# Two graph layers on one core: the start of layer 0's chain of norms, and the lead of layer 0 over layer 1

## The chip, the cores and the metric

The kernel runs on one core of one Trainium2 chip. The metric is the device time of one execution in microseconds (us); the time before is the median of three runs. Engines are named as in the profile: PE (matrix products), PEld (its weight loads), DVE (vector), ACT (scalar, activation functions), POOL and SP.

## The reference

The input `x` has 16 batches of 1024 rows of 256 values, `adj` 16 matrices of 1024 x 1024. Two layers follow each other, each wrapped in a residual and a norm. Cut to what matters here:

```python
# layer 0: 4 heads of 64 values
h = einsum('bnd,hde->bhne', x, W)
weight = sum over t of (adj == t+1) * (e_src[t] + e_dst[t])     # from h, a_src, a_dst
attention = softmax(where(adj == 0, -1e9, leaky_relu(weight)))
out = relu(attention @ h + bias) + h
out = layernorm over each head's 64 values
x = layernorm(x + out)
# layer 1: 8 heads of 32 values, no projections
n = layernorm(x)                      # gamma1, beta1
a = softmax(where(adj > 0, n n^T / sqrt(32), -inf)) @ n
x1 = x + a
mlp = gelu(layernorm(x1) @ W1 + b1) @ W2 + b2          # 256 -> 1024 -> 256
x = layernorm(x + (x1 + mlp))
```

Everything is in float32. Row b of `x` goes through both layers alone, so layer 0 of batch b+1 and layer 1 of batch b are independent.

## The kernel before

**Two streams.** `fast_path` is written as two Python generators, `layer0()` and `layer1()`, each of which runs over the 16 batches. A generator records instructions for the engines and then yields a cost in units of its own. Instructions of an engine run in the order in which they are recorded, so the order of these turns is the order of the work. A loop at the end of `fast_path` picks whose turn is next: layer 0's, if its place (batch plus fraction done, in units of `WORK0` = 47) is less than `wanted()`, otherwise layer 1's. `wanted()` reads a table, `COURSE`: for every point of layer 1's batch b (`ATTN1` = 82 units of attention, then 56 units of MLP up to `WORK1` = 138) it says how far layer 0 should be. It goes from 1.0 (batch b+1 not begun) to 2.0 (batch b+1 done), with 1.54 at the end of the attention, and 2.0 is reached 22 units ahead of the end of the MLP.

**Layer 0, a batch of it.** `prepare` loads rows in pairs of blocks of 128, transposes them (line 227), turns the adjacency into masks (lines 295 and 296) and makes the projections (line 322): 13 units. `attention0` runs 16 steps, (half n of the queries, head, half of the keys), of 2 units each. A step records its products (line 389, into a PSUM tile `acc`) and then the weights of the next step (line 374, into `p0`, four buffers, two a step). After a head's second step (`j4 == NB - 4`) its tail is due: `relu_residual` (lines 418 to 430).

**The chain of norms.** With a half's last head (head 3), `after0` goes on from `relu_residual` to the norms of these 512 rows. It is a chain of ten more parts, each of which waits for a number of units before it is recorded, so that its results are ready:

1. load of `xl`; sum and mean off, lines 445 and 446 (DVE)
2. squares `sq`, line 451 (ACT)
3. variances `v0s`, lines 454 and 455; the power `r0` on POOL, line 198; lines 457 and 458 (DVE)
4. scaling and residual, lines 460 and 461 (DVE)
5. statistics, lines 203 and 204, and `v2`, lines 469 and 470 (DVE); a second power on POOL
6. `t` and `ratio`, lines 208, 475 and 476 (DVE)
7. scaled rows into `sq` again, line 214 (ACT)
8. `x1`, line 484 (DVE); the first transposes, line 227 (PE), into `nT`, line 233 (ACT)
9. the second transposes, likewise
10. `v1`, line 494 (DVE)

`begin(chain, wait)` hangs a chain up at the running clock plus `wait`; `advance(cost)` moves the clock after each turn of either stream and runs the parts that are due. `complete(chain)` runs all that is left of one at once, without the pauses between the parts. `half(n)` in `layer1` calls it through `finish_norms` when layer 1 asks for half n of its batch, as only then must `x1`, `v1` and `nT` exist. Half 1 is asked for at the fifth step of a batch's attention.

**Layer 1, a batch of it.** `attention1` runs 32 steps of 2.5 units: scores (line 517), exponentials (line 522, ACT), one step later their masking (line 528, DVE), two steps later the products (lines 535 and 542). `heads_out` (lines 577 to 593) and `finish1` (lines 604 to 613) follow behind as chains. `mlp` runs four chunks of eight hidden blocks (lines 637 and 644, in pairs of 1.75 units) and eight output blocks (line 650, 3.5 units), each with a `last_norm` that adds the output block into `z` (line 680) and so frees one of two `po` tiles.

## Time and profile before

| what | value |
|---|---|
| median of three runs (lowest, highest) | 3886.35 us (3886.32, 3887.58) |
| span of the profiled run | 3880.2 us |
| mean granted TensorE clock | 0.957 |
| PE, PEld busy | 3451.0 us (89%), 2319.4 us (60%) |
| DVE, ACT, POOL busy | 2994.8 us (77%), 2151.8 us (55%), 388.3 us (10%) |
| HBM traffic over the span | 31 GB/s |
| chain that ended last, by engine | PE 64%, DVE 23%, issue 7%, POOL 3%, ACT 2%, DMA 1% |

Busy shares are means over the whole span. The kernel repeats one pattern, a batch of layer 1 beside the next batch of layer 0, fifteen times; between the start (layer 0 alone on the first batch) and the end (layer 1 alone on the last). One repetition takes about 237 us, so a microsecond in it is worth fifteen in the total. What limits the kernel differs from one part of the pattern to the next, so it is read with the timeline and with windows cut to those parts, not from the shares.

### The profile page before, as it was taken

The page shows a single profiled execution, that of the slowest core. Times are in us where ns is not written, and L with a number is a line of the kernel's source. Part 1 is how long each engine was busy: PE and PEld are TensorE (multiplying, and loading weights), DVE is VectorE, ACT ScalarE, POOL GpSimd, SP SyncE. Part 2 cuts the span into 40 slices and gives each one's busy share as a digit, 9 for nine tenths or more (in the row PEclk, how much of TensorE's full clock was granted, in tenths as well). Part 3 has the DMA queues.
Part 4 walks back from the last instruction along what each step waited for, and adds up shares of the span by engine and source line. Part 5 has one row for each costly group of instructions (what it writes and reads, how often), then busy time and mean ns, then how long its engine had stood idle before and what let it go on. Part 6 is the DMA issues. An engine that isn't in the chain of part 4 may idle for free.

```text
span 3880.2 us, 141934 instructions
## 1 busy us (share of the span) xinstructions
PE 3451.0 (89%) x64417; PEld 2319.4 (60%) x64417; DVE 2994.8 (77%) x5328; ACT 2151.8 (55%) x4732; POOL 388.3 (10%) x360
## 2 busy tenths in 40 slices
PE   5799898989989899898998989989898998989988
PEld 4457475565746657465584755747556574665746
DVE  4787796878868787797877968779687786878784
ACT  2564646647465464755646556464654746547454
POOL 0101001010110101101011010100101011010100
PEclk9799999999999999999999999999999999999999
DMA  4100101011020110201002010010101102010000
GB/s 100 34 14 23 35 12 41 8 31 27 13 44 4 34 25 15 43 4 38 19 18 40 11 37 14 23 35 12 41 8 31 27 13 44 4 31 14 14 6 13
DMA packets 77669, 97.67 MB, mean 25 GB/s; under 512 B 9088, under 2 KB 60160, under 8 KB 77056
## 3 DMA queue, kind: packets, MB, share of 16 engines
q0 software_dynamic: 18432, 33.56, 5.9%
q1 hardware_dynamic: 52736, 50.35, 4.2%
q8 instruction: 506, 8.29, 0.9%
q10 hardware_dynamic: 5888, 4.60, 0.4%
q14 instruction: 107, 0.88, 0.1%
HBM read 105.26 MB, written 16.78 MB: 31 GB/s over the span
## 4 chain that ended last, share of the span: by engine, by line
PE 64%; DVE 23%; issue 7%; POOL 3%; ACT 2%; DMA 1%; ACTq 0%; POOLq 0%; DVEq 0%
PE ps L517 14%; PE po L650 9%; PE acc L389 9%; PE po L535 9%; PE ps L637 8%; DVE p L374 7%; DVE p L528 6%; PE po L542 5%; PE acc L322 3%; POOL r L198 2%; PE acc L227 2%; DVE st L203 1%; PE acc L295 1%; PE ps L363 1%; DVE relu L421 1%
## 5 line engine op out<-in xcount | busy, mean ns | idle before, releaser
L528 DVE TENSOR_TENSOR p<-p,mask 128x1024 f32<-128x1024 f32 x1024 | 1199.0, 1221 | 175.0 <-ACT p L522 174.4
L522 ACT ACTIVATE p<-ps 128x512 f32<-128x512 f32 x2048 | 1058.8, 614 | 366.8 <-PE ps L517 364.8
L517 PE MATMUL ps<-nT 32*128 32x512 f32 x4096 | 748.6, 665 | 12.5 <-ACT cb L365 10.0
L374 DVE SCALAR_TENSOR_TENSOR p<-cb,dinv,mask 128x512 f32<-128x512 f32 x1024 | 698.9, 746 | 0.5 <-ACT cb L365 0.5
L389 PE MATMUL acc<-v,p 128*64 128x65 f32 x16384 | 577.9, 230 | 89.7 <-DVE p L374 87.4
L389 PEld LDWEIGHTS acc<-v,p 128*64 128x64 f32 x16384 | 532.6, 143 | 151.0 <-issue 102.4
L542 PEld LDWEIGHTS po<-v,p 128*32 128x32 f32 x32768 | 386.7, 109 | 326.5 <-issue 242.8
L535 PE MATMUL po<-p,v 128*32 128x512 f32 x2048 | 547.1, 609 | 25.0 <-DVE p L528 25.0
L535 PE MATMUL po<-p,unit 128*32 128x512 f32 x2048 | 546.6, 609 | 0.0
L637 PE MATMUL ps<-yT,w_sb 128*128 128x256 f32 x2048 | 480.3, 384 | 0.1
L650 PE MATMUL po<-w_sb,hid 128*128 128x256 f32 x2048 | 467.1, 383 | 0.0
L644 ACT ACTIVATE hid<-ps,b_sb 128x256 f32<-128x256 f32 x512 | 230.3, 471 | 380.8 <-PE ps L637 379.4
L650 PEld LDWEIGHTS po<-w_sb,hid 128*128 128x128 f32 x2048 | 389.5, 191 | 54.6
L637 PEld LDWEIGHTS ps<-yT,w_sb 128*128 128x128 f32 x2048 | 377.8, 190 | 73.1 <-issue 23.1
L542 PE MATMUL po<-v,p 128*32 128x33 f32 x32768 | 384.6, 198 | 2.2
L517 PEld LDWEIGHTS ps<-nT 32*128 32x128 f32 x4096 | 254.7, 191 | 154.7 <-ACT p L522 51.0
L535 PEld LDWEIGHTS po<-p,v 128*32 128x32 f32 x2048 | 78.2, 108 | 408.5 <-DVE p L528 219.0
L680 DVE TENSOR_TENSOR z<-po,x 128x256 f32<-128x256 f32 x128 | 54.1, 423 | 319.0 <-PE po L650 319.0
L198 POOL TENSOR_TENSOR r<-v,mhalf 128x1 f32<-128x1 f32 (+1 forms) x160 | 140.2, 877 | 1084.9 <-DVE v L684 616.0
L227 PE MATMUL acc<-ident,sq 128*128 128x128 f32 x136 | 37.0, 447 | 222.2 <-ACT sq L214 221.0
L214 ACT ACTIVATE sq<-hb,t,r 128x256 f32<-128x256 f32 x128 | 66.5, 590 | 256.3 <-DVE t L208 158.2
L198 POOL TENSOR_TENSOR r<-v1s,mhalf 128x4 f32<-128x4 f32 x32 | 54.4, 1701 | 1282.0 <-DVE v1s L609 1282.0
(116 smaller groups left out, 3149.5 us busy)
## 6 DMA issues: line engine op xcount, KB each, us to landing
ak<-in_adj_dram POOLq DMA_DIRECT2D x128, 256.0 KB, 3.8
xk<-in_x_dram SPq DMA_DIRECT2D x64, 256.0 KB, 2.7
xl<-in_x_dram SPq DMA_DIRECT2D x32, 512.0 KB, 3.9
out_dram<-z SPq DMA_DIRECT2D x128, 128.0 KB, 1.7
w_sb<-in_L_gnn_W_dram ACTq DMA_DIRECT2D x2, 1024.0 KB, 10.3
v<-in_L_gnn_a_src_dram ACTq DMA_DIRECT2D x1, 640.0 KB, 9.0
v<-in_L_gnn_a_dst_dram ACTq DMA_DIRECT2D x1, 640.0 KB, 3.8
w0e<-in_L_gnn_W_dram ACTq DMA_DIRECT2D x8, 32.0 KB, 7.7
```

What stands on the lines that cost most here:

```text
L198: nc.gpsimd.tensor_tensor(r, src, mhalf[:, :n], op=OP.pow)
L322: nc.tensor.matmul(ph, xT[:, c, g * P : (g + 1) * P], w0e[:, c, :], start=c == 0, stop=c == DC - 1)
L374: nc.vector.scalar_tensor_tensor(p[:, i, :], cb[:, hd % PAIR, :], dinv[:, j2 + i, hd : hd + 1], mask[n][:, j2 + i, :], op0=OP.max, op1=OP. ...
L389: nc.tensor.matmul(av[at : at + TILE, q, :], ps[i // 2][:, i % 2, q * P + at : q * P + at + TILE], v0[:, j4 + i, hd, :], start=j4 + i == 0 ...
L517: nc.tensor.matmul(tiles[e], of_keys[q, quad, keys], of_queries[q, quad, :], start=True, stop=True)
L522: nc.scalar.activation(p[:, i, :], tiles[e + i], AF.Exp, scale=SCALE1)
L528: nc.vector.tensor_mul(p, p, mask[n][:, jb, None, :].to_broadcast([P, PAIR, HALF]))
L535: nc.tensor.matmul(moved[at * Q : (at + 1) * Q, :], v, ps[0][:, e, :], start=jb == 0, stop=jb == NB - 1)
L542: nc.tensor.matmul(held[at : at + Q, q, e, :], ps[1][:, e, q * P + at : q * P + at + Q], values[:, hd, :], start=jb == 0 and e == 0 and q ...
L637: nc.tensor.matmul(ph, w1_sb[:, c, f * P : (f + 1) * P], yT[:, c, q * P : (q + GB) * P], start=c == 0, stop=c == DC - 1,)
L644: nc.scalar.activation(hid[f // 4][:, f % 4, :], ph, AF.Gelu, bias=b1_sb[:, f : f + 1], scale=1.0)
L650: nc.tensor.matmul(po, hid[f // 4][:, f % 4, g * P : (g + 1) * P], w2_sb[:, f, :], start=f == 0, stop=f == FC - 1,)
```

## The change

```diff
@@ attention0
             if j4 == 0 and i + 3 < len(steps) and hd % PAIR == PAIR - 1:
                 g = steps[i + 3][0], steps[i + 3][1] // PAIR
                 cbs[g] = spread_factor(*g)
-            yield 2.0
             if j4 == NB - 4:
                 norms[b, n, hd] = after0(b, n, hd, av, hb[n], rinv[:, n * BPH : (n + 1) * BPH, :])
-                begin(norms[b, n, hd], 0.0)
+                begin(norms[b, n, hd], 2.5)
+            yield 2.0
@@ fast_path
-    COURSE = [(0.0, 1.0), (ATTN1, 1.54), (WORK1 - 22.0, 2.0), (WORK1, 2.0)]
+    COURSE = [(0.0, 1.0), (ATTN1, 1.45), (WORK1 - 14.0, 2.0), (WORK1, 2.0)]
```

The first part moves the point at which a head's tail is hung up from the head of layer 0's next turn to the turn of the head's last products. The wait of 2.5 counts from the clock ahead of that turn's own 2.0 units, so the tail is recorded after whichever turn follows. The purpose is that the chain of the last head is not left until layer 0 is next given a turn.

The second part changes when layer 0 gets its turns. It is to be at 1.45 instead of 1.54 of its batch when layer 1's attention ends, and to be done 14 units ahead of the end of the MLP instead of 22. The instructions themselves, their number and their sizes stay as they are; only their order changes.

## The prediction

> **What bounds the kernel now.** I read the list of waits first, sorted by total, and looked only at PE rows, because PE has the largest busy share (89%). One row stands out; its columns are total us, times, longest us:

> ```profile
> PE acc L227 <- ACT sq L214: 221.0, 17, 15.6
> ```

> PE waits at the transposes of line 227 for the scaled rows `sq` (line 214), the seventh part of layer 0's chain of norms. Two of the 17 waits (7.27 and 9.62 us) belong to the start of the run, the other 15 to the fifteen changes from one batch of layer 1 to the next: 204 / 15 = 13.6 us each. The timeline of PE at one such change (start, duration, then the idle time in brackets):

> ```profile
> 619.63 0.62 PE L295 MATMUL acc<-identb,ak 128*128 128x128 bf16 x8
> 633.72 2.17 PE L227 MATMUL acc<-ident,sq 128*128 128x128 f32 x8 [13.47 <-ACT sq L214]
> 635.81 2.09 PE L517 MATMUL ps<-nT 32*128 32x512 f32 x8
> ```

> PE stands from 620.2 to 633.7 and then runs slowly: the four products of line 517 take 2.09 us here and 1.14 us a few microseconds later. What DVE does in that hole:

> ```profile
> 620.66 1.22 DVE L454 TENSOR_REDUCE v0s<-sq 128x16 f32<-128x1024 f32 x1
> 621.91 0.17 DVE L455 TENSOR_SCALAR v0s<-v0s 128x16 f32<-128x16 f32 x1
> ...
> 626.04 1.23 DVE L460 TENSOR_TENSOR hb<-hb,r 128x1024 f32<-128x1024 f32 x1 [1.33 <-POOL r L198]
> ...
> 632.86 0.16 DVE L208 SCALAR_TENSOR_TENSOR t<-mv,r 128x4 f32<-128x4 f32 x1 [1.80 <-POOL r L198]
> ...
> 636.93 4.63 DVE L528 TENSOR_TENSOR p<-p,mask 128x1024 f32<-128x1024 f32 x4
> ```

> It is one serial chain with two powers on POOL in it, and the masking that layer 1 needs (line 528) is queued behind it. Then I cut one batch (236.8 us) into four stages by what PE runs, and read busy time per stage (PE, PEld, DVE, ACT, POOL, then clock, DMA):

> ```profile
> 607.50:694.30 86.80, 71.17 (x1511) 37.34 (x1510) 65.02 (x95) 66.03 (x168) 10.43 (x11) 0.92 0.24 48
> 694.30:757.50 63.20, 58.44 (x1531) 33.59 (x1532) 59.18 (x86) 33.41 (x66) 1.94 (x1) 0.97 0.01 3
> 757.50:819.60 62.10, 59.70 (x873) 50.81 (x874) 56.51 (x128) 26.00 (x45) 9.66 (x6) 1.00 0.06 17
> 819.60:844.30 24.70, 24.70 (x120) 21.53 (x120) 5.82 (x24) 9.21 (x18) 2.23 (x4) 1.00 0.05 17
> ```

> Stage 1 (layer 1's attention beside layer 0's preparation) is PE's, apart from the hole. Stage 2 (both attentions) is DVE's: 59.2 of 63.2 us. Stage 3 (MLP beside layer 0's attention) loads both. Stage 4 (MLP alone) is PE's, with DVE idle three quarters of the time:

> ```profile
> 828.83 0.42 DVE L680 TENSOR_TENSOR z<-po,x 128x256 f32<-128x256 f32 x1 [7.38 <-PE po L650]
> 834.01 0.42 DVE L680 TENSOR_TENSOR z<-po,x 128x256 f32<-128x256 f32 x1 [3.01 <-PE po L650]
> 840.92 0.42 DVE L680 TENSOR_TENSOR z<-po,x 128x256 f32<-128x256 f32 x1 [4.73 <-PE po L650]
> ```

> [...] 0.50 granted from 627 to 637. [...] masking waits behind the chain. [...] from 737 to 747 PE reads 10.0 of 10 busy, yet the chain that ended last runs through DVE there. So below I price PE by the pieces of that chain, not by busy time: line 517 1.07 us a step, lines 535 and 542 1.00 + 0.56, one product step of layer 0 (line 389) 2.02, a pair of hidden blocks (line 637) 1.73, one output block (line 650) 3.45, line 322 1.09.

> **The change, part by part.** (a) *Where the chain begins.* Before, the code behind `yield 2.0` runs at layer 0's next turn. For the last head of a batch there is none until layer 1 has begun its next batch: COURSE ends at exactly 2.0, and the test is a strict "less than". The lead of 22 units that COURSE leaves therefore passes with the chain not begun; it begins in the hole's own batch, and ten units later `half(1)` completes it by force, seven parts in a row. After, it begins in the turn of the last products; 2.5 units is one turn of layer 1 later. The order of instructions of the changed kernel, built, shows this: the reductions, `sq`, the first power and lines 457 to 461 stand in front of the batch's last `z`; the statistics stand behind the first two masking operations of the new batch; only from line 208 (`t`) on is it forced, four parts.

> Price: PE waits from the end of its second set of products (619.3, without line 295's 0.6, which now comes later) for `t` behind the third masking (620.8 by the hole's rows), four line 214 operations behind the exponentials (2.08 us, the first two are enough), four transposes and the first `nT` (0.5 to 1.0). That is 3.5 us idle; bounds 2 (masking earlier) and 5.5 (all four scalings wanted first). Saved: 13.5 - 3.5 = 10. Slow clock: line 227 2.17 against twice 0.6, line 517 2.09 against 1.14, line 535 1.52 against 1.00, together 2.4, of which I keep 0.4. **Sum -12 us a batch.** The 8.6 us of DVE passes (seven of 1.22) and 1.1 us of ACT move to stage 4. That becomes 3 x 1.73 + 3 x 3.45 = 15.5 us long by (c), with about 4.2 us of `z` work (three groups of 1.4) and one `relu` of 1.45 on DVE: 14.3 in all, which just fits: nothing. The first power (3.82 us) lies beside an output block and its `z` there: nothing.

> (b) *`relu_residual` of the other heads* comes after one turn of layer 1 instead of after layer 0's next turn. It is a wait on the products of its head, with masking or weights queued behind it. But the next weights need those same products, because `p0` has four buffers, two a step. No new wait; no cost.

> (c) *COURSE.* Layer 0 owes 0.45 x 47 = 21.2 units at the end of layer 1's attention instead of 25.4; after 15 units of preparation that is 4 steps of products instead of 6, and the built order has 4 and 6. Three steps of layer 1's attention pass from stage 2 to stage 1. In front of the next batch are left 3 pairs of hidden blocks and 3 output blocks, before 6 and 4.

> Stage 1: +3 x (1.07 + 1.56) + 0.6 for transposes (line 593) = **+8.5**; DVE has room there. Stage 2, by DVE: three maskings of 2.31, two sets of weights of 2.65, one `relu` of 1.45 and the first half's `finish1` (about 5.5 in the rows at 696 to 705, which the built order has ahead of stage 2) leave: 6.9 + 5.3 + 1.45 + 4.4 (some of it stays) = **-18**, to 45 us. PE's own sum there is 10 x 1.07 + 12 x 1.56 + 4 x 2.02 + 2 x 1.05 + 1.6 = 41, so PE doesn't take over. Stages 3 and 4: PE sum before 16 x 1.73 + 8 x 3.45 + 10 x 2.02 + 4.5 = 80, measured 86.8, so 6.8 of friction; after, two more product steps, 84, with the same friction 90.8: **+4**. Of it stage 3 holds 68.5 of PE and 56.5 + 2 x 2.65 + 1.45 + 3 = 66 of DVE, so both are full; bounds 0 and +14.

> Sum: -12 + 8.5 - 18 + 4 = -17.5 us, fifteen times = -262. The first batch of layer 0 and the last of layer 1 run alone, unchanged. **3886 - 262 = 3624 us.**

> **Rivals.** *Boundary alone:* what stage 2 wins, stages 1 and 3 give back, as moving work between stages removes none. For it: stage 3 is nearly full on DVE already. Against: stage 4 has 18.9 us of DVE free. 3886 - 15 x 12 = 3706. *Collision in the MLP:* DVE passes of 1.2 us stand ahead of `z`, so the two `po` banks come free late and PE waits: stages 3 and 4 +14 in place of +4, -7.5 a batch, 3774. *Even better overlap:* friction halves where the engines are even: stage 2 44, stages 3 and 4 +1, -21.5 a batch, 3564. *Slower:* the forced rest still stops PE 7 us or more (-6), stage 2 gains 12, stages 3 and 4 lose 12 with 8.5 in stage 1: +2.5 a batch, 3924. Against it: both powers are done well before `t`, and nothing in the rows of `relu` shows DVE waiting.

> **How the numbers follow.** Forecast 0.52, boundary alone 0.22, better overlap 0.14, collision 0.08, slower 0.04. The range runs from 3555, which takes in the better overlap, to 3725, which takes in boundary alone; the collision and the slower case stay out. Faster by over 0.2%: all but the slower case and a little of the collision, 0.94; within 0.2%: 0.02; slower: 0.04.

> **What would show it.** In the waits, line 227 for `sq` falls from 221 to 60 us or so, and the clock's mean of 0.957 rises to 0.98. At a change of batch line 454 stands before the last `z`, and PE's idle time is under 6 us. DVE's idle times in stage 4 are filled. A batch lasts about 219 us. Wrong would be: PE idle of 7 us or more at the change; stage 2 longer than 50 us; PE waiting at line 650 for a `z`; PE waiting at line 389 for weights behind a `relu`.

## The result, and the profile after

The changed kernel takes 3661.73 us (four runs, 3660.5 to 3662.75) against 3886.34 us: a ratio of 0.9422, 95% interval 0.9406 to 0.9438. That is 224.6 us less, 15.0 us for each of the fifteen changes of batch; forecast were 262 and 17.5. The time lies inside the range.

First the busy shares, from the page of the changed kernel. Each engine is busy for as long as before to within 1% (DVE 2986.7 us against 2994.8, PE 3452.5 against 3451.0); it is the span that is shorter:

```profile
PE 3452.5 (94%) x64417; PEld 2304.6 (63%) x64417; DVE 2986.7 (82%) x5328; ACT 2156.0 (59%) x4732; POOL 384.5 (11%) x360
```

The row of the waits that carried the prediction (total us, times, longest us) has fallen from 221.0 to 51.2. Two long waits at the start of the run (7.03 and 9.96 us) make 17 of it, the fifteen changes of batch 2.3 us each:

```profile
PE acc L227 <- ACT sq L214: 51.2, 17, 10.0
```

The timeline of PE at one change of batch of the changed kernel (start, duration, idle time in brackets) shows the rest of the hole, and that slow matmuls behind it have stayed: 2.09 us for the scores and 1.06 for the first products. The last two rows are another change of the same run, with the same gap, behind which the scores take 1.14 us. The eight transposes take 1.9 us in both:

```profile
601.76 0.77 PE L542 MATMUL po<-v,p 128*32 128x33 f32 x64
604.81 1.94 PE L227 MATMUL acc<-ident,sq 128*128 128x128 f32 x8 [2.28 <-ACT sq L214]
606.73 2.09 PE L517 MATMUL ps<-nT 32*128 32x512 f32 x8
608.75 1.06 PE L535 MATMUL po<-p,v 128*32 128x512 f32 x1
...
1272.88 1.91 PE L227 MATMUL acc<-ident,sq 128*128 128x128 f32 x8 [2.28 <-ACT sq L214]
1274.81 1.14 PE L517 MATMUL ps<-nT 32*128 32x512 f32 x8
```

The granted clock (the column after the busy times) tells the two apart. It is halved for 3.41 us behind the first gap and stays full behind the second; of the fourteen changes that have a whole stage 1 behind them, eleven are like the first and three like the second:

```profile
606.57:609.98 3.41, 3.41 (x18) 0.92 (x20) 3.41 (x8) 2.60 (x7) 0.00 (x0) 0.50 0.00 0
1272.88:1278.30 5.42, 5.24 (x98) 2.87 (x99) 5.39 (x11) 5.37 (x12) 0.00 (x0) 1.00 0.23 53
```

DVE just ahead of it. The passes of the chain (lines 457 to 461) now stand ahead of the last `z` of the old batch, on both sides of the last but one, and `t` (line 208) has waited for nothing but its turn:

```profile
587.06 1.24 DVE L458 TENSOR_TENSOR xl<-xl,lnb_r 128x1024 f32<-128x1024 f32 x1
588.23 0.41 DVE L680 TENSOR_TENSOR z<-po,x 128x256 f32<-128x256 f32 x1
...
589.95 1.23 DVE L460 TENSOR_TENSOR hb<-hb,r 128x1024 f32<-128x1024 f32 x1 [0.44 <-POOL r L198]
591.21 1.23 DVE L461 TENSOR_TENSOR hb<-hb,xl 128x1024 f32<-128x1024 f32 x1
...
592.42 0.42 DVE L680 TENSOR_TENSOR z<-po,x 128x256 f32<-128x256 f32 x1
...
603.97 0.15 DVE L208 SCALAR_TENSOR_TENSOR t<-mv,r 128x4 f32<-128x4 f32 x1
```

One batch of the changed kernel in the four stages, columns as before (window, length, busy PE, PEld, DVE, ACT, POOL, clock, DMA):

```profile
589.94:677.80 87.86, 82.76 (x1755) 43.11 (x1754) 69.11 (x104) 72.56 (x182) 8.88 (x12) 0.98 0.24 47
677.80:723.03 45.23, 44.37 (x1221) 25.49 (x1221) 42.87 (x57) 27.24 (x52) 0.00 (x0) 1.00 0.01 4
723.03:796.12 73.09, 71.19 (x981) 60.35 (x981) 63.90 (x149) 29.05 (x53) 10.73 (x8) 1.00 0.05 16
796.12:811.80 15.68, 15.68 (x75) 13.54 (x75) 10.12 (x23) 6.05 (x10) 4.40 (x3) 1.00 0.05 18
```

Stage 2 has shrunk by 30%, stage 4 is two thirds full on DVE, and stage 1 is no shorter although most of its hole has gone. The border between stages 2 and 3 lies here at the first hidden block (line 637); the prediction's windows drew it one step of line 389 earlier, which makes its stage 2 about 2 us shorter and its stage 3 as much longer.

### The profile page after: what moved, and what is told of

Same layout as the page of the kernel before. It is cut to its first block, busy times and chain, and to the rows that moved or that the text cites. A ratio compares the mean times of both kernels' runs of the same rounds, so it can differ in the third digit from the quotient of the medians.

```text
span 3660.5 us, 142025 instructions
## 1 busy us (share of the span) xinstructions
PE 3452.5 (94%) x64417; PEld 2304.6 (63%) x64417; DVE 2986.7 (82%) x5328; ACT 2156.0 (59%) x4732; POOL 384.5 (11%) x360
## 4 chain that ended last, share of the span: by engine, by line
PE 63%; DVE 26%; issue 4%; ACT 3%; POOL 3%; DMA 1%; ACTq 0%; SPq 0%; DVEq 0%; POOLq 0%
PE ps L517 13%; PE po L535 10%; PE ps L637 9%; PE acc L389 9%; DVE p L528 7%; PE po L650 7%; PE po L542 6%; DVE p L374 6%; PE acc L322 3%; POOL r L198 3%; DVE st L203 2%; PE acc L295 1%; PE acc L227 1%; PE ps L363 1%; DVE mv L204 1%
## 5 line engine op out<-in xcount | busy, mean ns | idle before, releaser
L528 DVE TENSOR_TENSOR p<-p,mask 128x1024 f32<-128x1024 f32 x1024 | 1199.1, 1218 | 160.7 <-ACT p L522 156.9
L517 PE MATMUL ps<-nT 32*128 32x512 f32 x4096 | 769.1, 654 | 12.6 <-ACT cb L365 10.0
L389 PE MATMUL acc<-v,p 128*64 128x65 f32 x16384 | 556.4, 225 | 43.8 <-DVE p L374 42.7
L389 PEld LDWEIGHTS acc<-v,p 128*64 128x64 f32 x16384 | 511.5, 139 | 118.0 <-DVE p L374 65.2
L637 PE MATMUL ps<-yT,w_sb 128*128 128x256 f32 x2048 | 491.6, 387 | 0.7 <-issue 0.7
L650 PE MATMUL po<-w_sb,hid 128*128 128x256 f32 x2048 | 465.0, 381 | 0.0
L650 PEld LDWEIGHTS po<-w_sb,hid 128*128 128x128 f32 x2048 | 385.4, 190 | 64.0 <-issue 11.4
L637 PEld LDWEIGHTS ps<-yT,w_sb 128*128 128x128 f32 x2048 | 376.2, 191 | 64.3 <-issue 12.2
L517 PEld LDWEIGHTS ps<-nT 32*128 32x128 f32 x4096 | 268.0, 186 | 170.8 <-issue 56.8
L198 POOL TENSOR_TENSOR r<-v,mhalf 128x1 f32<-128x1 f32 (+1 forms) x160 | 158.1, 988 | 1009.2 <-DVE v L684 721.7
L296 ACT ACTIVATE mask<-acc,shift_c 128x1024 uint8<-128x1024 bf16 x128 | 144.3, 1127 | 44.3 <-PE acc L295 43.8
L322 PE MATMUL acc<-w0e,xT 128*128 128x264 f32 x512 | 146.2, 409 | 20.9 <-DVE hb L347 20.8
L278 POOL DMA_DIRECT2D ak<-in_adj_dram x128 | 69.7, 545 | 878.1 <-PE acc L295 864.7
L198 POOL TENSOR_TENSOR r<-v1s,mhalf 128x4 f32<-128x4 f32 x32 | 34.9, 1092 | 1132.2 <-DVE ranges L418 891.0
## 6 DMA issues: line engine op xcount, KB each, us to landing
w_sb<-in_L_gnn_W_dram ACTq DMA_DIRECT2D x2, 1024.0 KB, 10.2
```

The source lines that it names most:

```text
L198: nc.gpsimd.tensor_tensor(r, src, mhalf[:, :n], op=OP.pow)
L322: nc.tensor.matmul(ph, xT[:, c, g * P : (g + 1) * P], w0e[:, c, :], start=c == 0, stop=c == DC - 1)
L389: nc.tensor.matmul(av[at : at + TILE, q, :], ps[i // 2][:, i % 2, q * P + at : q * P + at + TILE], v0[:, j4 + i, hd, :], start=j4 + i == 0 ...
L517: nc.tensor.matmul(tiles[e], of_keys[q, quad, keys], of_queries[q, quad, :], start=True, stop=True)
L528: nc.vector.tensor_mul(p, p, mask[n][:, jb, None, :].to_broadcast([P, PAIR, HALF]))
L637: nc.tensor.matmul(ph, w1_sb[:, c, f * P : (f + 1) * P], yT[:, c, q * P : (q + GB) * P], start=c == 0, stop=c == DC - 1,)
```

## The experiments

All are read with one table: mean length in us of the four stages over fourteen batches of each profiled run (the first and the last batch of layer 1 are left out). Each ratio is to runs of the kernel before on the same chip. In PE's timeline stage 1 begins with the first scores (line 517) after an output block, stage 2 with the first line 363, stage 3 with the first line 637, and stage 4 at the end of the last line 389.

| kernel | time, us | ratio to before (95%) | stage 1 | stage 2 | stage 3 | stage 4 | batch |
|---|---|---|---|---|---|---|---|
| before | 3886.3 | 1 | 86.3 | 65.5 | 60.8 | 24.7 | 237.3 |
| changed | 3661.7 | 0.9422 (0.9406 to 0.9438) | 87.4 | 45.8 | 73.6 | 15.7 | 222.4 |
| e1 chain only | 3678.4 | 0.9456 (0.9440 to 0.9471) | 72.8 | 65.8 | 60.7 | 24.3 | 223.7 |
| e2 COURSE only | 3868.1 | 0.9946 (0.9930 to 0.9963) | 98.5 | 45.8 | 76.0 | 15.7 | 236.0 |
| e3 lead 22 | 3703.1 | 0.9523 (0.9507 to 0.9538) | 84.6 | 45.8 | 70.7 | 24.3 | 225.4 |
| e4 last head only | 3667.7 | 0.9432 (0.9416 to 0.9447) | 87.4 | 45.8 | 73.8 | 15.7 | 222.6 |
| e5 equal turns | 3636.6 | 0.9354 (0.9342 to 0.9367) | 85.4 | 45.8 | 74.2 | 15.7 | 221.0 |
| e6 finish1 split | 3760.0 | 0.9672 (0.9659 to 0.9685) | 86.0 | 52.7 | 74.3 | 15.7 | 228.7 |
| e7 slope 1.50, lead 18 | 3680.6 | 0.9468 (0.9454 to 0.9482) | 77.2 | 59.0 | 66.6 | 20.8 | 223.6 |
| e8 finish1 split, pause kept | 3750.6 | 0.9655 (0.9641 to 0.9668) | 86.0 | 48.8 | 78.1 | 15.7 | 228.6 |
| e9 e5 and lead 16 | 3608.9 | 0.9285 (0.9272 to 0.9298) | 85.3 | 45.8 | 72.2 | 15.7 | 219.0 |
| e10 lead 16 | 3646.8 | 0.9380 (0.9367 to 0.9393) | 87.8 | 45.8 | 72.2 | 15.7 | 221.4 |
| e11 e5 and lead 18 | 3645.8 | 0.9376 (0.9363 to 0.9388) | 83.8 | 45.9 | 72.6 | 19.1 | 221.4 |
| e12 e9, begun at once | 3584.5 | 0.9223 (0.9210 to 0.9235) | 84.1 | 45.7 | 72.2 | 15.7 | 217.6 |

### The two parts apart: e1 and e2

e1 is the changed kernel with the old table:

```diff
-    COURSE = [(0.0, 1.0), (ATTN1, 1.45), (WORK1 - 14.0, 2.0), (WORK1, 2.0)]
+    COURSE = [(0.0, 1.0), (ATTN1, 1.54), (WORK1 - 22.0, 2.0), (WORK1, 2.0)]
```

> Only the start of the chain moves; COURSE stays at 1.54 and a lead of 22. Theory A (the two parts pay in different places, and the lead of 22 was only useless because the chain had not begun): all but one part of the chain are recorded before layer 1 asks for the half, so PE's hole of 13.5 us at a change of batch goes wholly, with its slow clock: 13.5 to 15 us a batch, fifteen times, 3660 to 3685 us, near the time of the whole change. Theory B (a wait of about 2.3 us and the slow clock stay, as with both parts): 11 us a batch, 3720 us. Rival (the chain's passes on DVE in the MLP hold up the adds into z and PE with them): over 3760 us.

Measured 3678.4 us, theory A. Stage 1 falls by 13.5 us and no other stage moves by more than 0.4. The timeline of PE in e1, at the same place as above, has no idle time, and the granted clock of this stage is full:

```profile
602.37 0.66 PE L227 MATMUL acc<-ident,sq 128*128 128x128 f32 x4
603.85 2.49 PE L517 MATMUL ps<-nT 32*128 32x512 f32 x8
```

The 13.5 us are PE's idle time alone (15.6 us of stage 1 before, 2.2 in e1). PE's busy time there stays at 71 us, although the slow clock has gone: the scores beside the chain are recorded at up to 2.49 us all the same. What they wait for was not followed.

Five parts of the chain lie in stage 4 here: of its 24.4 us DVE is busy 16.2, before 5.8, at no cost to the stage.

e2 is the kernel before with the new table:

```diff
-    COURSE = [(0.0, 1.0), (ATTN1, 1.54), (WORK1 - 22.0, 2.0), (WORK1, 2.0)]
+    COURSE = [(0.0, 1.0), (ATTN1, 1.45), (WORK1 - 14.0, 2.0), (WORK1, 2.0)]
```

> Only COURSE changes (1.45, lead 14); the chain still begins at layer 0's next turn. Theory A: the hole of 13.5 us stays fifteen times, since the chain does not begin in the lead whatever its length; stage 2 (both attentions) falls from 63 to about 45 us, stage 1 grows by 11 to 13, MLP stages by 2 to 4: 2 to 5 us a batch, 3810 to 3856 us. Rival (the two parts only pay together): 3886 us or more, with stage 2 unchanged.

Measured 3868.1 us, 0.5% less than before and 12 us above what theory A allowed. The hole is there, 228.5 us in all, the same 17 times:

```profile
PE acc L227 <- ACT sq L214: 228.5, 17, 15.0
```

Stage 2 gives 19.7 us, stage 1 takes 12.2 and stages 3 and 4 take 6.2 of it: 1.3 us a batch are left. The product of the two ratios, 0.9456 x 0.9946 = 0.9405, agrees with 0.9422 within the intervals, so the parts add. **The move of `begin` carries the gain; the new table adds a few tenths of a per cent.**

### The lead and the other heads: e3 and e4

e3 is the changed kernel with the lead back at 22 (`WORK1 - 22.0`, slope 1.45).

> Chain begins early as in the changed kernel, COURSE at 1.45, but the lead back at 22. Theory A (what is left of the hole, 2.3 us of idle PE and about 2 us of slow clock, goes once five parts of the chain lie ahead of the new batch; the MLP stage takes its steps in less time with a little more friction): 2 to 4 us a batch below the changed kernel, 3600 to 3632 us. Rival (the shorter stage of MLP with layer 0 becomes DVE's, and the longer MLP alone leaves DVE idle again): 3 us a batch or more above it, 3705 us or more.

Measured 3703.1 us: the rival's outcome to within 2 us, 41 us above the changed kernel, and 25 us above e1. The hole's rest does go (stage 1 -2.8), but stages 3 and 4 grow from 89.3 to 95.0. The twelve steps of layer 0 stand closer together in stage 3, and it is the order that hurts, not capacity. In this window of e3, which ends 2 us ahead of the stage, neither engine is full, DVE at 59.7 of 68.9 us:

```profile
731.30:800.20 68.90, 63.11 (x886) 52.70 (x884) 59.71 (x137) 26.25 (x46) 10.21 (x7) 0.98 0.05 15
```

Two rows of e3's waits have grown (the changed kernel has 105.4 and 42.7 us in them). DVE stands at `z` for an output block, PE stands for weights:

```profile
DVE z L680 <- PE po L650: 189.9, 98, 7.3
...
PE acc L389 <- DVE p L374: 98.7, 53, 5.0
```

Sorted by stage, only the second one costs time. PE's wait for weights is all in stage 3, 5.6 us a batch instead of 1.9, and stage 3 has 3.4 us at half clock instead of 1.2; together these are about 4.8 of the 5.7 us. The wait at `z` has grown in stage 4 (4.9 us for 1.3), where PE is busy without a pause (26.60 of 26.60 us from 800.2 to 826.8) and the idle DVE cost nothing.

e4 begins only head 3's tail early; the others are left where they were:

```diff
-            if j4 == NB - 4:
+            if j4 == NB - 4 and hd == H0 - 1:
                 ...
                 begin(norms[b, n, hd], 2.5)
             yield 2.0
+            if j4 == NB - 4 and hd < H0 - 1:
                 ...
+                begin(norms[b, n, hd], 0.0)
```

> As the changed kernel, but only head 3's tail is begun early; the relu tails of heads 0 to 2 wait for layer 0's next turn as before. Theory A (their place costs and brings nothing, because the next weights wait for the same products): 3662 us within 6. Rival (an earlier relu frees its PSUM tile earlier and that is part of the gain): 3690 us or more. Other rival (the earlier relu delays masking): 3640 us or less.

Measured 3667.7 us, all four stages as in the changed kernel: the place of the other heads' `relu_residual` is worth nothing that can be told.

### Where stage 1 went: e5, e6 and e8

e2 had shown stage 1 growing by 12.2 us for three more steps of attention, where the prediction had 8.5. The chain that ended last, of the changed kernel, suggests why (start, duration, piece; the second scores have no preparation between them and the products before):

```profile
623.03 1.09 PE acc L322 x4
624.12 1.07 PE ps L517 x8
625.19 1.00 PE po L535 x8
626.19 0.56 PE po L542 x60
626.75 1.73 PE ps L517 x7
628.48 0.99 PE po L535 x8
```

Behind a projection or a mask the scores take 1.07 us; straight behind the products they take 1.73. My reading was that the four score tiles are still being read by ACT's exponentials (2.07 us a step). In the built order the kernel before has one such bare step in stage 1, the changed one five: at the new slope a mask and a projection often fall into the same gap, and the next gap stays empty. e5 spaces them evenly:

```diff
             turn_mask(k)
-            yield 0.5
+            yield 0.7
...
-                yield 0.9
+                yield 0.7
...
                     turn_mask(k + 1)
-                    yield 0.5
+                    yield 0.7
```

> The changed kernel, with layer 0's preparation cut into equal turns (0.7 units for a mask and 0.7 for a projection, instead of 0.5 and 0.9; same sum), so that they fall into different steps of layer 1's attention. The number of steps in stage 1 that have no preparation between their scores and the previous products falls from 5 of 22 to 2. Theory A (stage 1 came out 3.4 us longer than reckoned because a bare step costs about 0.75 us more: the four score tiles are still being read by the exponentials): stage 1 shorter by about 2.3 us, 3662 - 34 = 3628 us, range 3610 to 3645. Theory B (the excess is the burst of finish1 on DVE that has moved into stage 1): unchanged, 3655 to 3668 us.

Measured 3636.6 us, theory A: three bare steps fewer, stage 1 shorter by 1.9 us, the other stages within 0.5. That a bare step costs more is thereby shown; that it waits for ACT fits the rows (in the one above ACT's exponentials end at 627.3, and the scores at 628.5) but was not tried by itself.

e6 tests the rival, `finish1`'s burst on DVE (line 604 and the statistics):

```diff
         nc.vector.tensor_add(o, o, x1)
         mv = ...
+        yield 1.25
         for g in range(BPH):
             statistics(o[:, g, :], mv[:, g, :])
...
         t = minus_mean(mv[:, :, 0], r, BPH)
-        yield 1.5
         scale_shift(o, o, t, r, BPH)
```

> The changed kernel, with finish1's burst on DVE cut in two: the residual add and the statistics are recorded in different turns, with one masking between, and the pause ahead of its scaling is left out in exchange. Theory A (bare steps are the excess in stage 1): within 10 us of 3662. Theory B (the burst holds masking and PE for about 3 us in stage 1): 3662 - 45 = 3617 us, range 3600 to 3640.

Measured 3760.0 us, outside both. Stage 1 lost 1.4 us, stage 2 gained 7.0. ACT's timeline in e6 shows the pause that I had left out at work: the scaling of `o` is recorded right behind `t`, waits 3.86 us for it, and `cb` and the exponentials are queued behind it:

```profile
687.23 2.07 ACT L522 ACTIVATE p<-ps 128x512 f32<-128x512 f32 x4 [0.39 <-PE ps L517]
693.16 2.08 ACT L214 ACTIVATE o<-o,t,r 128x256 f32<-128x256 f32 x4 [3.86 <-DVE t L208]
695.14 0.35 ACT L343 COPY esr<-acc 128x256 f32<-128x256 f32 x1
695.39 1.07 ACT L365 ACTIVATE cb<-ps 128x512 f32<-128x512 f32 x2
```

e8 keeps that pause and leaves out the one between the adds into `x1` and `t`:

```diff
+        yield 1.25
         for g in range(BPH):
...
         nc.vector.tensor_add(x1, x1, o)
-        yield 2.0
         t = minus_mean(mv[:, :, 0], r, BPH)
         yield 1.5
```

> As e6 (finish1's residual add and statistics in different turns), but with the pause between t and the scaling kept; the pause between the adds into x1 and t is left out instead. Theory A (e6 lost 7 us in stage 2 because ACT stood 3.9 us at the scaling of o for t, with the exponentials of cb and p queued behind it, and the burst was never worth more than the 1.8 us that stage 1 then lost): stage 2 back at 45 to 47, stage 1 at 86, 3662 - 25 = 3637 us, range 3625 to 3665. Rival (splitting the burst itself costs stage 2): 3720 us or more.

Measured 3750.6 us: a miss, with the rival's number. Most of stage 2's loss is gone (48.8 against 52.7), so e6's pause was worth about 4 us of its 7. But stage 3 is now 4.5 us longer, where ACT again stands for `t` (93.1 us over the run in that row of its waits, 47.5 in the changed kernel).

In both runs about half of the loss is slow clock. Stage 2 of e6 has 4.1 us more of idle PE a batch and 8.1 us at half clock (none in the changed kernel); stage 3 of e8 has 2.2 us more of idle PE and 6.1 us at half clock instead of 1.2. The burst itself is worth the 1.4 us that stage 1 lost in both: PE's waits at lines 322 and 535 there, 1.5 us a batch in the changed kernel, are gone. The pauses that had to be moved to make room for the split cost several times that.

### Other points of the table: e7, e9, e10, e11

e7: slope 1.50 and lead 18.

> The changed kernel with COURSE at 1.50 and a lead of 18, between those of before and after. Bare steps in stage 1: 0 of 20. Theory A (bare steps cost 0.75 us each; the hole's rest of 2.3 us goes in part; stage 2 takes back 6 to 7 us by two more steps of both attentions, stage 1 loses two steps of 2.6 us; MLP stages 1 to 2 us less friction than at 22): stage 1 about 78, stage 2 about 53, MLP stages about 88: 219 us a batch, 3662 - 45 = 3617 us, range 3590 to 3650. Rival (only the sum of DVE's work counts and the split does not matter): 3655 to 3680 us.

Measured 3680.6 us: the rival's number by a hair, but not its reason. Stage 1 fell by 10.2 us as expected, stage 2 took back 13.2 where I had reckoned 6 to 7, and stages 3 and 4 fell by 1.9. Two steps of layer 1 and one of layer 0 moved into stage 2. By the prediction's prices they are 7.3 us for PE; the rest is mostly PE's idle time there, 5.5 us a batch instead of 1.1, most of it for masking and for line 584 on DVE.

e9 is e5 with a lead of 16, e10 the changed kernel with a lead of 16, e11 is e5 with a lead of 18.

> e5's equal turns, and a lead of 16 in place of 14 (slope 1.45 kept). The parts of the chain that are forced at the new batch stay four, as one more output block of the MLP follows the last products of layer 0. Theory A (a longer lead only pays when it takes a forced part away; it shortens the stage in which DVE is full): stage 1 unchanged at 85.5, stage 4 longer by 1.7 to 3.5, stage 3 shorter by less: 3637 us to 3675 us. Rival (the lead shortens the hole's rest): 3600 to 3630 us.

> The changed kernel with a lead of 16 alone (turns of the preparation as they were). The built order behind the last products is the same as at 14, only the order within stage 3 differs. Theory A (equal turns act in stage 1, the lead in stage 3, so they add): e9 less e5 is -28 us, so 3662 - 28 = 3634 us, range 3620 to 3648. Rival (the lead paid only together with equal turns): 3655 us or more.

> e9 with a lead of 18: one more output block follows the last products of layer 0, and the statistics of the chain fall ahead of the new batch, so three parts are forced in place of four. Theory A (this takes the hole's rest away, 2.3 us idle and about as much slow clock, as at a lead of 22, where stage 1 was 3 us shorter; stage 3 with DVE full gives part back): stage 1 at 82 to 84, stages 3 and 4 at 88 to 91, 3570 to 3625 us. Rival (stage 3 is held by DVE, so every unit of lead beyond 16 goes straight into the time, as at 22): 3640 us or more.

e9 measured 3608.9 us, below theory A's range, and not for the rival's reason: stage 1 and stage 4 are e5's. From 14 to 16 nothing changes behind the last products; only the turns within stage 3 are dealt differently, and it is 1.9 us shorter. PE's waits for weights at line 389 are 31.5 us over the run instead of 43.0, 0.7 us a batch, and the 2.4 us a batch at half clock that e5 has in stage 3 are gone. e10 measured 3646.8 us, inside its range, though the two do not simply add: the lead alone is worth 15 us, with equal turns 28. e11 measured 3645.8 us, the rival: one part fewer is forced and stage 1 falls to 83.8 us as expected, but stages 3 and 4 rise from 87.9 to 91.7.

### A better kernel: e12

If a longer lead is dear in stage 3, the chain itself can be begun sooner. e12 is e9 with

```diff
-                begin(norms[b, n, hd], 2.5)
+                begin(norms[b, n, hd], 0.0 if (n, hd) == (NH - 1, H0 - 1) else 2.5)
```

> e9 with the wait of the last head of half 1 at 0 in place of 2.5, so that its relu is recorded in the very turn of its products and the whole chain one turn earlier; the turns of both streams, and so stage 3, stay as in e9. The statistics then stand ahead of the new batch's masking, t behind the second masking in place of the third. Theory A (the hole's rest is set by how far the chain has come at the new batch, and stage 4's DVE has room for one more part): stage 1 shorter by 1.5 to 3 us with PE's idle time under 1.5 us, 3609 - 33 = 3576 us, range 3560 to 3590. Rival (the second power on POOL and the four scalings on ACT stand in series in any case, or the passes now hold up the last z): 3600 us or more.

Measured 3584.5 us, theory A and the fastest kernel of the study: 302 us below the kernel before, 77 below the changed one. Stages 2 to 4 are e9's, and PE's idle time at the change is 1.10 us instead of 2.28. Stage 1 is shorter by 1.2 us on average, less than expected, and has not one length but three, about 82.9, 84.4 and 85.5 us; the section on the hardware takes that up.

## Why the prediction was right, and where it was off

**The mechanism** was right: the chain was not begun in the old lead; begun earlier, it takes the hole away. e1 shows it alone, 13.5 us a batch in stage 1 and nothing elsewhere. The sign, the place and the number of forced parts are as written, but they start with the scaling (line 214): DVE has line 347 between `t` and line 484, so `t` had come in its own turn.

**Step (a), -12 us.** In the changed kernel the chain's part in stage 1 is 98.5 - 87.4 = 11.1 us (e2 against the changed kernel). Two errors nearly cancelled, which is luck. PE's idle time is 2.3 us and not 3.5. But of the slow clock, which was priced at 2.4 us with 0.4 kept, more stays: stage 1 is 86.2 us long behind the three changes without it and 87.4 to 87.8 behind the eleven others, 1.2 us on average. The price itself was too high, too, as it counted the transposes, which take 1.9 us at full clock.

**Step (a), the passes in stage 4 at nothing:** right. Its length is 15.7 us, 15.5 by the sum. **Step (b):** right, by e4.

**Step (c), stage 2, -18:** measured -19.7. **Stages 3 and 4, +4:** measured +3.9, from 85.4 to 89.3, but not by the table alone. That costs 6.2 us there (e2); the earlier chain gives 2.4 back, with 1.8 us less of PE's waiting for weights. The prediction had no such term, so this agreement is luck as well.

**Step (c), stage 1, +8.5:** this is the term that was most mis-sized. It measured +12.2 (86.3 to 98.5 in e2). I took 1.07 us for the scores of each added step from rows in which preparation work stood ahead of them. Added steps have none to stand ahead, as the same preparation is now dealt to 22 steps instead of 19: the five bare steps of stage 1 take 1.7 to 2.1 us each for their scores, where the kernel before has one of 1.85, so they are dearer than reckoned by about 3.2 us in all. Another 0.5 us is the hole, which is longer in e2 (13.98 us against 13.47). That is about the 3.7 us. e5 gives 1.9 us back by dealing the same work evenly. `finish1`'s burst, which I placed in stage 1 at nothing, does cost 1.4 us there (e6, e8), but the kernel before had a wait of 1.6 us at line 322, for line 584, that is gone, so the zero came out right for another reason.

**The sum.** -11.1 + 12.2 - 19.7 + 3.9 = -14.7 us by these figures, against -17.5 forecast; the run gave -15.0. The time lies about midway between the forecast and boundary alone (3706 us). That rival had the better idea of the table's worth, since e2 brings only 18 us where the forecast had 5.5 us a batch, 82 in all; it gave the chain 12 us a batch, where alone it brings 14.

**The signs that were named.** Idle time at the change under 6 us, clock at 0.98 (0.985), line 454 ahead of the last `z`, stage 4 filled: all seen. A batch of 219 us: 222.4.

## What to carry to other kernels

Where work is recorded by turns, ask of every chain not only how long it has but at whose turn it begins: a lead of any length is worth nothing to a chain that starts on the other side of it. A step priced from a row carries its neighbours with it: the same scores took 1.07 us here behind a projection, and 1.73 straight behind the products. And before two streams are rebalanced, price the stage that the work goes to by the order there, not by its idle share: of the 19.7 us that stage 2 gave in e2, the other stages took 18.4.

## What the runs showed of the hardware

I had expected the slow clock to go with most of the idle time. Here it did not scale with it: behind 2.28 us of idle PE the scores still take 2.09 us at eight of the fourteen changes of the changed kernel. In e12 the idle time is 1.10 us at each of the fourteen changes, and the clock falls after some of them and not after others. Two changes of e12, PE's timeline:

```profile
2552.48 1.93 PE L227 MATMUL acc<-ident,sq 128*128 128x128 f32 x8 [1.10 <-ACT sq L214]
2554.88 2.09 PE L517 MATMUL ps<-nT 32*128 32x512 f32 x8 [0.47 <-ACT nT L233]
...
2771.75 1.90 PE L227 MATMUL acc<-ident,sq 128*128 128x128 f32 x8 [1.10 <-ACT sq L214]
2774.15 1.14 PE L517 MATMUL ps<-nT 32*128 32x512 f32 x8 [0.50 <-ACT nT L233]
```

The granted clock (the column after the busy times) in windows behind the first and behind the second:

```profile
2553.00:2557.00 4.00, 3.43 (x18) 1.18 (x22) 3.99 (x10) 3.21 (x8) 0.00 (x0) 0.65 0.12 37
2557.00:2561.00 4.00, 4.00 (x84) 2.43 (x88) 3.39 (x3) 2.33 (x5) 0.01 (x1) 0.50 0.00 0
...
2772.00:2776.00 4.00, 3.35 (x24) 1.20 (x26) 3.99 (x10) 4.00 (x10) 0.00 (x0) 1.00 0.10 33
2776.00:2780.00 4.00, 4.00 (x156) 2.39 (x148) 3.92 (x5) 3.98 (x9) 0.53 (x1) 1.00 0.28 29
```

The first batch has a stage 1 of 85.5 us, the second of 82.8. Over e12's fourteen batches the granted clock stays full at six changes (stage 1 of 82.8 to 83.2 us), is halved for 3.41 us at four (84.3 to 84.5) and for 6.83 us at four (85.5 to 85.8). A fall of the clock cost stage 1 here 1.5 or 2.7 us, more than the 1.10 us of idle time before it.

A gap of 1.10 us, with 1.9 us of transposes behind it, was thus followed by half clock at eight of e12's fourteen changes: it was not safe by its length. What ties a fall to a place in the grid was not shown. e1, with no gap at this place, keeps the full clock there (1.00 from 594.0 to 666.8).
